# One-hot matrices over 80 nodes instead of 128, address loads moved in the first layer, and more tiles copied in place of gathered

## The chip, the cores and the metric

The kernel runs on one core of one Trainium2 chip. The metric is the device time of one execution in microseconds (us). Five engines of the core work side by side, each on its own queue of instructions, and meet only at semaphores: TensorE (PE, matmuls and transposes), VectorE (DVE), ScalarE (ACT), GpSimd (POOL, which here only issues gathers) and SyncE (SP, which issues the plain transfers). Times are compared with three runs of the kernel before.

## The reference, cut to what matters

Two graph layers over 12,500 nodes with 128 features, and 200,000 edges that are sorted by their target node. All of it is 32-bit floating point.

```python
# layer 0
h = relu(layernorm(x))
agg = segment_sum(h[src], dst, 12500)          # sum of the sources of each node's edges
x = x + (agg @ W_rel.T + b_rel + h @ W_root.T)
# layer 1
h = relu(layernorm(x))
w = silu(edge_features @ We1 + be1) @ We2 + be2   # one vector of 128 for each edge
agg = segment_sum(h[src] * w, dst, 12500)
x = x + h + (silu(agg @ Wn1 + bn1) @ Wn2 + bn2)
```

## The kernel before, in words

**Groups and tiles.** The edges are cut into 196 groups of 1024, and a group into 8 tiles of 128 edges (one edge for each partition). Each layer walks the groups in order. Because the edges are sorted by target, the 1024 edges of a group go to few neighbouring nodes: with the inputs of the reference the widest group spans 72 of them. The kernel takes a window of `W` nodes from the first target of the group on, and checks on the chip that no edge lies outside it (a slow second program follows if one does).

**Sum over edges.** For each group VectorE compares the targets with the numbers 0 to `W`-1 (`compare`, line 278) and so makes a one-hot matrix `oh` of 128 edges by `W` nodes for each tile. PE multiplies each tile of source rows `hs` (the weights) by its one-hot matrix (line 391) and accumulates the 8 tiles in one bank: 128 features by `W` nodes. In the profile each of these 32-bit products stands as two matmuls and two weight loads. VectorE adds the bank to the sums `both` at the window's place (`add`, line 409), whose address comes from a register.

**Source rows: gathered or copied.** POOL gathers the rows of a tile by index from chip memory (`fetch`, line 265, one instruction for one tile), into one of 6 buffers `hs`. It may not start on a buffer before the scatter that read it 6 groups ago is done. Some tiles are not gathered. The transposed table of all nodes lies in `both`, a node to a column; ScalarE and VectorE copy 128 columns, one instruction for one column of 128x4 bytes, into a tile `hc` (lines 608 and 606; three such tiles), PE transposes it (`turn`, line 633), and ScalarE copies the result into `hs` (`place`, line 639). I call this a helped tile. `HELP` tells how many: in layer 0 one in each group (from group 18 on, after a start in which the first rows are normalized as they come), in layer 1 nine in ten groups. `HC` splits the 128 columns: in layer 0 VectorE takes 60 and ScalarE 68, in layer 1 56 and 72. The tile's columns are copied four groups (`HW`) ahead of the group that needs it.

**Addresses.** The place of each column is read into registers, up to 16 (`HL`) with one load instruction on the engine that copies (`take`, line 591); then follow the copies (`put`). In layer 1, `hook` lets VectorE issue one such load right behind the compare, one behind the addition of line 376 and one behind the product of line 380, so that they run beside these; the copies come later, in `spread`. In layer 0 there are no hooks: `spread` alternates loads and copies behind `add`.

**Layer 1.** For each group PE makes the hidden layer of the edges (`hidden`, line 355), ScalarE its silu (line 358), PE the weights of the messages (`weigh`, line 368), VectorE adds a bias (line 376) and multiplies by the source rows (line 380); then comes the scatter of line 391. PE's order in one step is hidden of group g+2, scatter of g, weigh of g+1, then a `turn` and node work.

**Node work.** As soon as the sums of 512 nodes (a batch; there are 25) are complete, their dense part is done between the groups: in layer 0 matmuls of lines 471 and 475, statistics on VectorE (lines 483, 289, 292) and ScalarE (294, 308); in layer 1 lines 545, 547, 555 to 564.

**What sets the order.** All semaphores and the order on each engine are written out by hand; `beside` and `plan` place the node work and the turns behind certain groups. An engine executes strictly in this order, so a wait on an engine holds all behind it.

Of the kernel before, what the change touches and what calls it, by code (L numbers as in the profile page):

```python
# [20 lines left out]
D = 128  # L21
GT = 8
GE = GT * P
W = 128
WG = 512
GL = 4
NB = 4
# [4 lines left out]
XB = 4  # L32
FB = 4
EP = 51
HELP = ((1, 1), (9, 10))
HC = (60, 56)
HW = 4
TABLE = 16512
HL = 16
# [27 lines left out]
def helped(n_nodes, n_edges):  # L67

    ng = n_edges // GE
    nbt = len(last_groups(n_nodes, n_edges))
    layers = []
    for begin, (tiles, groups) in ((min(ng, -(-nbt // 2) + FB) + 1, HELP[0]), (1, HELP[1])):
        ends = (begin - 1 - -(i + 1) * groups // tiles for i in range(ng * tiles // groups))
        layers.append((begin, [(e + HW, e) for e in ends if e + HW < ng - 1]))
    return layers


# [21 lines left out]
def kernel(  # L102
# [41 lines left out]
    FG = min(NG, -(-NBT // 2) + FB)  # L144
    places, blocks = help_places(N, n_edges)
    helps = [
        (layer, h, e, begin, j)
        for layer, (begin, groups) in enumerate(helped(N, n_edges))
        for j, (h, e) in enumerate(groups)
    ]  # L150
    helped_groups = {(layer, h) for layer, h, *_ in helps}

    def rows_of(ap, n0, rows, nt):
        return ap[n0 : n0 + rows * nt, :].rearrange("(t p) d -> p t d", p=rows)
# [36 lines left out]
    with (  # L191
# [64 lines left out]
        def fetch(layer, g):  # L256

            k = layer * NG + g
            at(G, done["src", 0 if g < 8 else 1], done.get(("ap", k - (HB if g < NG - 8 else LB))))
            if layer:  # L260
                at(G, *(done["h1 out", b] for b in range(max(0, NBT - 2), NBT)))
            elif g >= FG:
                at(G, *(done["h0 out", b] for b in range(max(0, NBT - 3), NBT)))
            for t in range(tiles_of[g] - ((layer, g) in helped_groups)):
                ins = G.indirect_dma_start(  # L265
                    out=hs[k % HB][:, t, :], out_offset=None,
                    in_=h1_d if layer else x if g < FG else h0_d,
                    in_offset=bass.IndirectOffsetOnAxis(
                        ap=src_sb[:, g * GT + t : g * GT + t + 1], axis=0
                    ),  # L270
                )
                done["hs", k] = inc(ins, f"hs{k % HB}", 16)
# [339 lines left out]
        def spread(layer, g):  # L612

            for taken in hooked:
                put(V, taken)
            hooked.clear()
            for engine, rest in ((V, hooks), (A, list(chunks(layer, g, A)))):
                for chunk in rest or (chunks(layer, g, V) if engine is V and not layer else ()):
                    put(engine, take(engine, chunk))
            hooks.clear()  # L620

# [10 lines left out]
            at(T, done["b3"] if layer else done.get(("placed", i - 2)), done["table", NBT - 1])  # L632
            done["tile", i] = inc(T.transpose(bank, hc[i % 3], ident), "pe")  # L633

        def place(i, layer, h):
# [3 lines left out]
            done["hx", k] = done["placed", i] = inc(A.copy(hs[k % HB][:, GT - 1, :], bank), "act")  # L639
            if layer:  # L640
                done["b3"] = done["placed", i]

        with tc.tile_critical():
# [112 lines left out]
            for i, (layer, h, e, begin, j) in enumerate(helps):  # L756
# [6 lines left out]
                if not layer:  # L763
                    plan(0, e + 2, lambda i=i, h=h: place(i, 0, h))
            placed = {e + 1: (i, 1, h) for i, (layer, h, e, *_) in enumerate(helps) if layer}
# [8 lines left out]
            for layer in range(2):  # L774
                fetch(layer, 0)
                if layer:
                    weigh(0)
                else:
                    done["oh", 0] = inc(compare(0, 0), "dve")
                for g in range(NG):  # L780
                    k = layer * NG + g
                    if g + 1 < NG:
                        fetch(layer, g + 1)
                    if not layer:
                        if g + 1 < NG:
# [12 lines left out]
                    else:  # L798
                        if g:
                            add(1, g - 1)  # L800
                        if 2 * EG <= g + 3 < NG and (g + 3) % EG == 0:
                            load(g + 3)
                        if g + 2 < NG:
                            hidden(g + 2)
                        scatter(1, g)
                        hooks.extend(chunks(1, g, V))
                        if g + 1 < NG:
                            weigh(g + 1)
                    for what in beside[layer].get(g, ()):
                        what()  # L810
                    spread(layer, g)
                    if layer and g in placed:
                        place(*placed[g])
                add(layer, NG - 1)
                for what in beside[layer].get(NG, ()):
                    what()
# [191 lines left out]
```

## Time and profile before

| | us |
|---|---|
| kernel before, median of 3 runs (4913.62 to 4926.87) | 4920.62 |
| the profiled execution | 4865.67 |
| its span, first to last instruction | 4863.9 |
| layer 0 from group 18 on, and layer 1 without its ends: the stretches read below | 400 to 2200, 2600 to 4600 |
| ScalarE busy | 3051.0 (63%) |
| VectorE busy | 2750.9 (57%) |
| GpSimd busy | 2629.1 (54%) |
| PE matmuls busy | 2554.6 (53%) |

A line of the grouped view holds line, engine, operation, tiles written and read, shapes, count; then busy time and mean duration in ns of one; then the engine's idle time just before these instructions and what ended it. "issue" means that nothing that the profile shows was waited for. A line of the timeline holds start, duration, what was done and how often, and in brackets the idle time before it. PEclk is the granted TensorE clock as a share of the full one.

### The profile page before, as it was taken

Reading aid. Unit: us, or ns where it says so; the run is one execution under the profiler, and the core shown is the slowest. Engines: PE = TensorE matmul, PEld = TensorE weight load, DVE = VectorE, ACT = ScalarE, POOL = GpSimd, SP = SyncE. Lnnn points to the kernel's source line nnn. Section 1 sums busy time; section 2 is a strip of 40 time slices with the busy share of each in tenths; the row PEclk is TensorE's granted clock in tenths of the full one; section 3 lists DMA queues with packets and bytes.
Section 4 is the critical chain, followed back from the end, with each engine's and each line's share of the span. In section 5 each row is a group of like instructions: output and inputs, shape, how many; then the busy total and the mean of one; then the engine's idle time right before and its main releaser. Section 6 shows DMA issues by size and latency. Waiting matters only on the chain.

```text
span 4863.9 us, 77667 instructions
## 1 busy us (share of the span) xinstructions
PE 2554.6 (53%) x11440; PEld 1986.8 (41%) x11440; DVE 2750.9 (57%) x21943; ACT 3051.0 (63%) x24975; POOL 2629.1 (54%) x2791
## 2 busy tenths in 40 slices
PE   2433333333333333334456767677666776667777
PEld 1423333332332333333344545455444554444555
DVE  3545555555455555555256566666655665666665
ACT  4646656666666666667356666666666666666664
POOL 6655555555555555554555455555554555555544
PEclk9666655566556666656677777777777777777778
DMA  3411111111111111111122222212221222222221
GB/s 109 112 49 50 51 43 47 47 52 46 44 45 53 45 45 53 47 47 43 52 63 58 59 62 63 59 55 61 64 58 55 59 61 59 63 61 61 58 57 48
DMA packets 187106, 275.72 MB, mean 57 GB/s; under 512 B 48331, under 2 KB 136658, under 8 KB 181586
## 3 DMA queue, kind: packets, MB, share of 16 engines
q0 software_dynamic: 89088, 182.63, 14.5%
q1 hardware_dynamic: 97300, 87.96, 5.9%
q14 instruction: 429, 3.51, 0.2%
q8 instruction: 93, 1.52, 0.1%
q10 hardware_dynamic: 196, 0.09, 0.0%
HBM read 244.89 MB, written 25.60 MB: 56 GB/s over the span
## 4 chain that ended last, share of the span: by engine, by line
ACT 33%; issue 28%; DVE 16%; PE 11%; another core or an unknown queue 8%; ACTq 3%; DVEq 1%; SPq 0%; DMA 0%
ACT hc L608 28%; DVE hc L606 9%; PE bank L391 4%; ACT hid L358 3%; PE pair L355 3%; ACTq L591 3%; DVE oh L278 2%; PE pair L368 2%; DVEq L591 1%; DVE stn L289 1%; ACT hs L639 1%; PE bank L475 1%; DVE st L289 0%; DVE hs L380 0%
## 5 line engine op out<-in xcount | busy, mean ns | idle before, releaser
L265 POOL DMA_INDIRECT hs<-h_d,src_sb x2648 | 2499.4, 944 | 2137.2 <-PE bank L391 1119.3
L608 ACT COPY hc<-both 128x4 uint8 x23936 | 2596.6, 190 | 1364.9 <-issue 1344.9
L606 DVE TENSOR_TENSOR hc<-both,bank 128x4 uint8<-128x4 uint8 x19840 | 1588.2, 150 | 1238.9 <-issue 1226.3
L391 PE MATMUL bank<-oh,hs 128*128 128x128 f32 x6252 | 1268.7, 386 | 291.1 <-issue 120.1
L391 PEld LDWEIGHTS bank<-oh,hs 128*128 128x128 f32 x6252 | 1194.4, 294 | 525.5 <-issue 264.2
L633 PE MATMUL pair<-ident,hc 128*128 128x128 f32 x172 | 73.0, 424 | 1281.1 <-ACT hc L608 411.5
L355 PE MATMUL pair<-ef,we_sb 50*128 50x512 f32 (+1 forms) x782 | 549.8, 837 | 75.8 <-ACT hid L358 33.5
L633 PEld LDWEIGHTS pair<-ident,hc 128*128 128x128 f32 x172 | 30.4, 176 | 1318.9 <-issue 778.5
L278 DVE TENSOR_TENSOR oh<-bank,rel 128x1024 f32<-128x1024 f32 x392 | 475.0, 1212 | 16.9 <-issue 16.7
L376 DVE TENSOR_TENSOR pair<-pair,be_sb 128x1024 f32<-128x1024 f32 x196 | 240.3, 1226 | 407.6 <-PE pair L368 214.9
L368 PE MATMUL pair<-we_sb,hid 128*128 128x128 f32 x3126 | 441.6, 302 | 4.7 <-issue 4.7
L368 PEld LDWEIGHTS pair<-we_sb,hid 128*128 128x128 f32 x3126 | 434.9, 222 | 3.0 <-issue 3.0
L358 ACT ACTIVATE hid<-pair,be_sb 128x1024 f32<-128x1024 f32 x196 | 217.1, 1108 | 105.5 <-remote 58.9
L355 PEld LDWEIGHTS pair<-ef,we_sb 50*128 50x128 f32 x782 | 172.7, 244 | 260.2 <-issue 222.4
L380 DVE TENSOR_TENSOR hs<-pair,hs 128x1024 f32<-128x1024 f32 x196 | 239.3, 1221 | 17.6 <-DMA hs<-h_d,src_sb 8.1
L633 PE MATMUL bank<-ident,hc 128*128 128x128 f32 x170 | 58.6, 345 | 353.6 <-remote 87.1
L633 PEld LDWEIGHTS bank<-ident,hc 128*128 128x128 f32 x170 | 26.2, 154 | 391.6 <-issue 137.9
L265 POOL DMA_INDIRECT hs<-in_x,src_sb x136 | 128.5, 945 | 73.2 <-issue 40.2
L409 DVE TENSOR_TENSOR both<-both,bank 128x128 f32 x392 | 109.0, 278 | 71.8 <-remote 47.1
L483 DVE TENSOR_TENSOR bank<-bank,xt 128x512 f32<-128x512 f32 (+1 forms) x25 | 17.2, 689 | 153.7 <-PE bank L475 52.9
L294 ACT ACTIVATE sdn<-mvn,eps 128x4 f32<-128x4 f32 (+1 forms) x50 | 14.9, 298 | 125.0 <-DVE mvn L292 45.6
L555 PE MATMUL bank<-bn_r,ones_r 1*128 1x512 f32 (+1 forms) x50 | 37.8, 845 | 90.0 <-remote 60.7
(69 smaller groups left out, 888.9 us busy)
## 6 DMA issues: line engine op xcount, KB each, us to landing
hs<-h_d,src_sb POOLq DMA_INDIRECT x2648
ef<-in_ef_t SPq DMA_DIRECT2D x98, 408.0 KB
xt<-in_x SPq DMA_DIRECT2D x48, 256.0 KB
h_d<-h SPq DMA_DIRECT2D x48, 256.0 KB
keep_d<-xt SPq DMA_DIRECT2D x24, 256.0 KB
xt<-keep_d SPq DMA_DIRECT2D x24, 256.0 KB
out_x<-xt SPq DMA_DIRECT2D x24, 256.0 KB
hs<-in_x,src_sb POOLq DMA_INDIRECT x136
```

Source lines behind the costliest of these rows:

```text
L265: ins = G.indirect_dma_start(out=hs[k % HB][:, t, :], out_offset=None, in_=h1_d if layer else x if g < FG else h0_d, in_offset=bass.Indire ...
L278: return V.tensor_tensor(oh[k % OB][:, :n, :], io.unsqueeze(1).to_broadcast([P, n, W]), rel[:, g, :n].unsqueeze(2).to_broadcast([P, n, W]) ...
L355: ins = T.matmul(hp_b[:, c : c + m], we1_sb, e[:, c : c + m], start=True, stop=True)
L358: ins = A.activation(hid[g % 2][:, :n], hp_b[:, :n], AF.Silu, bias=be1_sb)
L368: ins = T.matmul(wp[:, t, :], hid[g % 2][:, t * P : (t + 1) * P], we2_sb, start=True, stop=True)
L376: ins = V.tensor_add(w, w, be2_sb.unsqueeze(1).to_broadcast([P, n, D]))
L380: done["msg", g] = inc(V.tensor_mul(h, w, h), "dve")
L391: ins = T.matmul(ap[k % AB], hs[k % HB][:, t, :], oh[k % OB][:, t, :], start=(t == 0), stop=(t == tiles_of[g] - 1),)
L591: _, columns = nc.values_load_multi_w_load_instructions(help_at[row : row + 1, block, lo:hi], engines=[kind], min_val=TABLE, max_val=TABLE ...
L606: ins = V.tensor_tensor(to, column, zero_b, ALU.bitwise_or)
L608: ins = A.copy(to, column)
L633: done["tile", i] = inc(T.transpose(bank, hc[i % 3], ident), "pe")
```

## The change

The window shrinks from 128 to 80 nodes: `oh`, the bank and the addition are over 80 columns, and so is the moving side of the scatter's matmuls. In layer 0, VectorE's chunks of columns are handed to the hooks before the compare of the next group, and one address load is issued right behind that compare, ahead of `add`; the rest is as before. The helped tiles go from 1 in each group to 11 in ten groups in layer 0 (so that in each tenth group two of the eight tiles are copied and six gathered) and from 9 in ten to 19 in twenty groups in layer 1. The split becomes 64 and 64 columns in layer 0, 60 (VectorE) and 68 (ScalarE) in layer 1. `slot` counts which tile from the end of the group a helped tile is.

```diff
-W = 128
+W = 80
-HELP = ((1, 1), (9, 10))
-HC = (60, 56)
+HELP = ((11, 10), (19, 20))
+HC = (64, 60)
...
-        ends = (begin - 1 - -(i + 1) * groups // tiles for i in range(ng * tiles // groups))
-        layers.append((begin, [(e + HW, e) for e in ends if e + HW < ng - 1]))
+        ends = [begin - 1 - -(i + 1) * groups // tiles for i in range(ng * tiles // groups)]
+        slots = [ends[:i].count(e) for i, e in enumerate(ends)]
+        layers.append((begin, [(e + HW, s, e) for s, e in zip(slots, ends) if e + HW < ng - 1]))
...
-            for t in range(tiles_of[g] - ((layer, g) in helped_groups)):
+            for t in range(tiles_of[g] - helped_groups.count((layer, g))):
...
-                for chunk in rest or (chunks(layer, g, V) if engine is V and not layer else ()):
+                for chunk in rest:
...
-            done["hx", k] = done["placed", i] = inc(A.copy(hs[k % HB][:, GT - 1, :], bank), "act")
+            done["hx", k] = done["placed", i] = inc(A.copy(hs[k % HB][:, GT - 1 - slot, :], bank), "act")
...
                     if not layer:
+                        hooks.extend(chunks(0, g, V))
                         if g + 1 < NG:
                             compared = compare(0, g + 1)
+                            hook()
```

Counted in the two programs: 189 helped tiles instead of 172 in layer 0 and 179 instead of 170 in layer 1, 2758 gathers instead of 2784, 22,836 column copies on VectorE instead of 19,840 and 24,268 on ScalarE instead of 23,936, 1711 address loads on VectorE instead of 1405 and 1788 on ScalarE instead of 1767.

More of the change, by code (lines that the diff above doesn't have):

```diff
@@ L146 @@
     helps = [
-        (layer, h, e, begin, j)
+        (layer, h, slot, e, begin, j)
         for layer, (begin, groups) in enumerate(helped(N, n_edges))
-        for j, (h, e) in enumerate(groups)
+        for j, (h, slot, e) in enumerate(groups)
     ]
-    helped_groups = {(layer, h) for layer, h, *_ in helps}
+    helped_groups = [(layer, h) for layer, h, *_ in helps]
     def rows_of(ap, n0, rows, nt):
@@ L633, in turn, with place @@
             done["tile", i] = inc(T.transpose(bank, hc[i % 3], ident), "pe")
-        def place(i, layer, h):
+        def place(i):
+            layer, h, slot, *_ = helps[i]
             bank = b3[:, :P] if layer else tp[i % 2][:, 0, :]
@@ L755 @@
                 plan(1, ready[0] - 1, lambda b=b: node_load(b, keep_d))
-            for i, (layer, h, e, begin, j) in enumerate(helps):
+            placed = {}
+            for i, (layer, h, _, e, begin, j) in enumerate(helps):
                 tiles, groups = HELP[layer]
@@ L762 @@
                 plan(layer, e + 1, lambda i=i, layer=layer: turn(i, layer))
-                if not layer:
-                    plan(0, e + 2, lambda i=i, h=h: place(i, 0, h))
-            placed = {e + 1: (i, 1, h) for i, (layer, h, e, *_) in enumerate(helps) if layer}
+                if layer:
+                    placed[e + 1] = i
+                else:
+                    plan(0, e + 2, lambda i=i: place(i))
             plan(0, FG, check_a)
@@ L812 @@
                     if layer and g in placed:
-                        place(*placed[g])
+                        place(placed[g])
                 add(layer, NG - 1)
@@ L969, in by_tile @@
         return np.pad(v, (0, pad), constant_values=fill).reshape(-1, P).T
-    helps = [h for _, groups in helped(a["x"].shape[0], n_edges) for h, _ in groups]
+    helps = [
+        (h + 1) * GT - 1 - slot
+        for _, groups in helped(a["x"].shape[0], n_edges)
+        for h, slot, _ in groups
+    ]
     places, blocks = help_places(a["x"].shape[0], n_edges)
     help_t = np.zeros((P, blocks[-1], P), np.int32)
-    for place, h in zip(places, helps):
-        help_t[place] = a["src"][(h + 1) * GE - P : (h + 1) * GE]
+    for place, t in zip(places, helps):
+        help_t[place] = a["src"][t * P : (t + 1) * P]
     arrays = {
```

## Prediction

> **What bounds the kernel now.** I read the windows view first, to set the two layers apart, then each engine's groups in each layer with the idle time before them, then a timeline.
>
> ```profile
> 400.00:2200.00 1800.00, 647.58 (x2987) 585.47 (x2986) 983.28 (x9528) 1167.05 (x10464) 989.16 (x1050) 0.61 0.18 47
> 2600.00:4600.00 2000.00, 1385.22 (x6103) 990.72 (x6104) 1234.08 (x8668) 1311.07 (x10636) 1063.00 (x1128) 0.74 0.22 60
> ```
>
> The columns are the stretch, then busy time of PE, weight loads, VectorE, ScalarE, GpSimd, then the granted clock. No engine is busy over 70%. Layer 0 has 150 compares in this stretch, 12.0 us a group; layer 1 has 159, 12.6 us a group. The groups of ScalarE and VectorE in layer 0:
>
> ```profile
> L608 ACT COPY hc<-both 128x4 uint8 x10200 | 1107.2, 190 | 575.8 <-issue 567.1
> L294 ACT ACTIVATE sdn<-mvn,eps 128x4 f32<-128x4 f32 x19 | 5.6, 297 | 37.1 <-DVE stn L289 16.7 <-DVE mvn L292 15.6 <-issue 4.7
> ```
>
> ```profile
> L606 DVE TENSOR_TENSOR hc<-both,bank 128x4 uint8<-128x4 uint8 x9000 | 735.5, 150 | 674.8 <-issue 668.3
> L278 DVE TENSOR_TENSOR oh<-bank,rel 128x1024 f32<-128x1024 f32 x150 | 182.4, 1216 | 14.8 <-issue 14.8
> L409 DVE TENSOR_TENSOR both<-both,bank 128x128 f32 x150 | 41.2, 275 | 0.0
> L483 DVE TENSOR_TENSOR bank<-bank,xt 128x512 f32<-128x512 f32 x19 | 13.3, 700 | 116.7 <-remote 46.5 <-PE bank L475 45.5 <-issue 24.7
> ```
>
> ScalarE is busy 1167 us and idle 567 us before column copies for nothing that is shown; real waits come to some 40 us. So its 12 us are full. VectorE has the same kind of idle time and really waits only at L483 (117 us, 0.78 us a group). Counted off tile by tile (60 copies on VectorE and 68 on ScalarE make one), ScalarE finished last in all 172 tiles of layer 0, at the median by some 4 us. ScalarE sets layer 0.
>
> In layer 1:
>
> ```profile
> L608 ACT COPY hc<-both 128x4 uint8 x10314 | 1121.2, 190 | 604.4 <-issue 595.9
> L358 ACT ACTIVATE hid<-pair,be_sb 128x1024 f32<-128x1024 f32 x159 | 176.5, 1110 | 19.2 <-issue 11.8 <-PE pair L355 7.2
> L639 ACT COPY hs<-bank 128x128 f32<-128x128 f32 x143 | 36.6, 256 | 11.1 <-issue 11.0
> L547 ACT ACTIVATE hid<-bank,bn_sb 128x512 f32<-128x512 f32 x20 | 13.7, 687 | 54.5 <-PE bank L545 33.1 <-remote 14.9 <-PE pair L368 3.3
> ```
>
> ```profile
> L376 DVE TENSOR_TENSOR pair<-pair,be_sb 128x1024 f32<-128x1024 f32 x159 | 195.5, 1230 | 281.7 <-PE pair L368 177.7 <-issue 51.6 <-remote 35.3
> ```
>
> Again ScalarE is the fullest, with 85 us of waits (L547, L358, L639) for PE. VectorE has room: 282 us of waiting at L376.
>
> The idle time called "issue" is the odd part. A timeline of layer 1 shows what goes with it:
>
> ```profile
> 3666.60 0.38 ACT L608 COPY hc<-both 128x4 uint8 x3 [1.14 <-issue]
> 3668.04 0.19 ACT L608 COPY hc<-both 128x4 uint8 x1 [0.52 <-issue]
> ...
> 3669.76 6.44 ACT L608 COPY hc<-both 128x4 uint8 x64
> ...
> 3680.01 0.69 ACT L547 ACTIVATE hid<-bank,bn_sb 128x512 f32<-128x512 f32 x1 [2.63 <-PE bank L545]
> ```
>
> ```profile
> 3666.97 0.94 POOL L265 DMA_INDIRECT hs<-h_d,src_sb  x1 [0.31 <-issue]
> 3677.59 0.94 POOL L265 DMA_INDIRECT hs<-h_d,src_sb  x1 [9.68 <-PE bank L391]
> ```
>
> ```profile
> 3669.66 0.45 PE L633 MATMUL bank<-ident,hc 128*128 128x128 f32 x1 [8.49 <-DVE hc L606]
> 3670.04 3.78 PE L355 MATMUL pair<-ef,we_sb 50*128 50x512 f32 x4
> 3673.75 3.57 PE L391 MATMUL bank<-oh,hs 128*128 128x128 f32 x16
> 3677.16 1.95 PE L368 MATMUL pair<-we_sb,hid 128*128 128x128 f32 x16
> ```
>
> While gathers run, the copies come in ones and threes with steps of 0.7 us; while GpSimd pauses, 64 columns take 6.44 us, 0.101 us each, addresses included. In all such runs of seven gathers the copies go freely during the first three or four and stall some 80% of the time during the rest and 1.5 us after. So the last gather of a run costs both copying engines about 1 us each.
>
> **The change part by part**, for each group.
>
> *ScalarE, layer 0.* 11/10 tiles of 64 columns are 70.4 instead of 68: 2.4 x 0.101 = +0.24. A tenth more of a place (L639, 0.26 us): +0.03. A tenth less of a gather: from its mean share (567 us by 1050 gathers, 0.54 us) to its whole 1.25 us step; I take 1.0, since it is the last of a run that goes: -0.10. [...] The rows show ScalarE stalling with the gathers, and I follow them. Sum +0.17, by 172 groups **+29 us**.
>
> *VectorE, layer 0.* 70.4 columns instead of 60, at 0.072 us (32 in 2.29 us in the same timeline, GpSimd idle): +0.75. Its loads of addresses go from 4.0 to 5.2 a group; one that isn't covered shows as a gap of 0.54 us: +0.65. The first load now lies beside the compare; before, it was uncovered in about a third of the groups, for 0.77 us: -0.27. It is also ahead of `add`'s wait now; it waits for nothing itself, and nothing but `add` stands behind it. The compare over 640 instead of 1024 elements: L278 takes 1.216 us and 512 elements took 0.70 (L483), so 0.82: -0.40. The addition over 80: from 275 to some 225 ns, -0.05. Gather -0.10. Sum +0.58. It is hidden by the 4 us by which VectorE is ahead and by its 0.78 us at L483; 0.2 us of rate is left. If that cover fails, up to 0.58 x 172 = 100 us come. I take 0.1 us a group: **+17 us**.
>
> *PE.* The scatter's 16 matmuls ran cold in 3.57 us, 223 ns each; warm ones of the same shape (L368) took 122. With 80 instead of 128 columns streamed the cold ones would take 139: -1.34 us; the other end is nothing, if the weight loads, which stay 128x128, set the pace. [...] I take 0.8 us a scatter.
>
> Where does it go? In layer 0 PE mostly stands at L633 for ScalarE's columns; what a faster scatter gives is that the sums of a batch (L475, then L483, then L294) come sooner: L294's wait is 37.1 / 19 = 2 us a batch, and 22 batches lie here: **-18 us**. In layer 1, L547 waits 54.5 / 20 = 2.7 us a batch behind hidden, scatter and weigh: 24 x 0.8 = **-19 us**. L358 and L639 wait 30 us in this stretch, 36 in the layer; a third: **-12 us**. The wait at L376 is VectorE's and doesn't count while ScalarE is full.
>
> *Layer 1, the rest.* ScalarE copies 64.6 columns instead of 64.8 (-0.02) and a twentieth of a gather goes (-0.05): 0.07 x 191 = **-13 us**. VectorE: 6.6 columns more, +0.48; compare and addition -0.45; half a load more, mostly under the three hooks, +0.1: inside its 1.8 us a group at L376.
>
> *Start.* 17 groups, bound by gathers of 8 tiles and by the normalization; 0.2 us each: **-4 us**. The pause between the layers and the last groups have no helped tiles and stay.
>
> Sum: 29 + 17 - 18 - 19 - 12 - 13 - 4 = **-20 us** on the profiled 4865.67. That execution is 1.1% under the median of the runs; the same difference on 4920.62 gives **4900 us**.
>
> **The rivals.**
>
> *VectorE becomes the bound of layer 0* (18%). It takes on 0.58 us a group and has 0.78 of waiting, part of which can't go: after a batch's sums PE needs scatter and L471 to L475, 5 us or more behind the turn. It decides from the point where VectorE's columns end last. Then all 0.58 us count, 100 us in place of 29 + 17 - 18: +52 us, 4973. For it: 1.2 more loads and 10.4 more columns. Against it: it was never last in 172 tiles.
>
> *The scatter gets no faster, or its gain isn't passed on* (14%): weight loads bind. The PE terms go (49 us): +29, 4950.
>
> *PE's order is the loop of layer 1* (18%). The timeline has PE 8.5 us at L633 and then four steps one after the other, with VectorE (6 us) and GpSimd (9.7 us) behind it. If a sooner scatter releases all, half of the 0.8 us counts in 195 groups, -78 in place of -31, and 0.2 us in layer 0, -34 in place of -18: -83, 4837; with the full cold gain, 4790. Against it: ScalarE is at 95% with its stalls.
>
> *It does next to nothing* (8%): all within 15 us.
>
> **How the numbers follow.** The case that I summed has 42%: 4900, its own range 4855 to 4930 (ends of the PE term and of the last gather). Within 0.3%, some 15 us, is about what a measurement of this kernel can't tell from no change. Of the summed case six in ten lie below 4906 and nearly all others in the band. Faster: 0.42 x 0.62 + 0.18 + 0.02 = 0.46. Slower: 0.18 + 0.13 + 0.02 = 0.33. Same: 0.21. The range from 4810 to 4985 leaves out the far ends of the PE loop and of a bound VectorE.
>
> **What would show it.** Right: ScalarE still last in nearly all tiles of layer 0; L608's idle time per gather as before, its copies up by 332; L391's 16 matmuls in some 2.2 us when cold; L278 at about 0.82 us; L547's and L294's idle time down by a third; layer 0 at 12.0 to 12.2 us a group, layer 1 at 12.3. Wrong: VectorE last in layer 0 and PE's L633 released by L606; matmuls of L391 still 220 ns apart; gathers that run on without pauses, so that the stalls no longer clear.

## The result, and the profile after

| | before | after |
|---|---|---|
| median of 4 runs each, us | 4917.29 (4913.62 to 4926.87) | 5056.52 (5045.29 to 5076.2) |
| ratio of the medians, 95% interval | | 1.0284 (1.0243 to 1.0326): slower |
| the profiled execution, us | 4865.67 | 5046.45 |
| its span, us | 4863.9 | 5044.3 |
| layer 0, us a group | 11.83 | 12.62 |
| layer 1, us a group | 12.50 | 12.71 |

The last two rows are the distance between the additions of two groups (18 and 190 in layer 0, 2 and 188 in layer 1), over the number of groups between. 172 groups by 0.79 us are 136 us, 186 by 0.21 are 39: together 175 of the 180 us by which the spans differ. The profiled execution of before was 1.1% below its median and that of after at the lower end of its runs, so the spans differ by more than the medians (180 and 139 us).

Line numbers shift by a few with each edit: the scatter is L391, L393 or L394, the column copies are L606 to L611, weigh is L368, L370 or L371, the turn L633 to L636.

The windows of the changed kernel, over the same two stretches (columns as before: PE, weight loads, VectorE, ScalarE, GpSimd, granted clock):

```profile
400.00:2200.00 1800.00, 676.94 (x2808) 592.56 (x2808) 984.35 (x10446) 1137.98 (x10211) 923.50 (x977) 0.51 0.17 44
2600.00:4600.00 2000.00, 1492.81 (x6035) 1114.22 (x6033) 1225.01 (x9619) 1289.70 (x10459) 1047.62 (x1108) 0.68 0.21 59
```

The clock fell, 0.61 to 0.51 and 0.74 to 0.68, and PE was busier for less work: 1493 us instead of 1385 in layer 1. Layer 0 has 141 groups in its stretch instead of 150, one in 12.77 instead of 12.0 us.

The groups of ScalarE, VectorE and PE in layer 0 (400 to 2200 us) after the change:

```profile
L610 ACT COPY hc<-both 128x4 uint8 x9947 | 1080.2, 190 | 561.2 <-issue 553.2
L296 ACT ACTIVATE sdn<-mvn,eps 128x4 f32<-128x4 f32 x18 | 5.3, 297 | 85.7 <-DVE mvn L294 63.6 <-issue 11.8 <-DVE stn L291 10.3
```

```profile
L608 DVE TENSOR_TENSOR hc<-both,bank 128x4 uint8<-128x4 uint8 x9948 | 809.8, 150 | 681.7 <-issue 666.8 <-PE bank L393 5.6 <-remote 2.8
L280 DVE TENSOR_TENSOR oh<-bank,rel 128x640 f32<-128x640 f32 x141 | 115.3, 817 | 21.9 <-issue 21.9
L411 DVE TENSOR_TENSOR both<-both,bank 128x80 f32 x141 | 33.1, 234 | 24.5 <-issue 21.9 <-PE pair L635 0.9 <-DVE hc L608 0.3
L485 DVE TENSOR_TENSOR bank<-bank,xt 128x512 f32<-128x512 f32 x18 | 12.6, 700 | 67.3 <-PE bank L477 29.3 <-issue 20.9 <-PE pair L635 7.5
```

```profile
L393 PE MATMUL bank<-oh,hs 128*128 128x80 f32 x2256 | 503.1, 416 | 384.9 <-DVE both L411 237.0 <-remote 62.6 <-issue 46.7
L635 PE MATMUL pair<-ident,hc 128*128 128x128 f32 x156 | 68.2, 437 | 658.6 <-remote 260.0 <-ACT hc L610 187.5 <-ACT hs L642 131.7
```

The same two rows of the kernel before, not shown until now; its scatter has no wait at all:

```profile
L391 PE MATMUL bank<-oh,hs 128*128 128x128 f32 x2400 | 511.4, 402 | 0.0
L633 PE MATMUL pair<-ident,hc 128*128 128x128 f32 x151 | 64.1, 424 | 1126.9 <-ACT hc L608 338.0 <-remote 335.8 <-ACT hs L639 335.2
```

Three readings. PE's scatter now waits 237 us (1.7 us a group) for VectorE's addition, where before PE stood only at the turn; PE's wait at both together is about as long (1127 us before, 1044 after), so it is who ends the wait that has changed. (The kernel waits there for one VectorE semaphore that stands for the addition and for the compare ahead of it.) ScalarE waits 85.7 us instead of 37.1 for the statistics, which VectorE makes too. And the scatter over 80 columns takes as long as over 128 (mean record 416 ns, 402 before).

In layer 1, two rows of PE, for before (first, 2600 to 4600 us) and after (2700 to 4700 us):

```profile
L391 PE MATMUL bank<-oh,hs 128*128 128x128 f32 x2544 | 493.2, 372 | 105.2 <-issue 63.3 <-DVE hs L380 41.8
L368 PE MATMUL pair<-we_sb,hid 128*128 128x128 f32 x2544 | 357.1, 301 | 0.0
```

```profile
L393 PE MATMUL bank<-oh,hs 128*128 128x80 f32 x2512 | 505.1, 384 | 152.2 <-issue 90.5 <-DVE hs L382 61.3
L370 PE MATMUL pair<-we_sb,hid 128*128 128x128 f32 x2515 | 475.7, 368 | 0.0
```

By the group (16 matmuls), weigh went from 2.25 to 3.03 us although nothing in it was changed, and the scatter, which was to get faster, from 3.10 to 3.22. The timeline shows one such pair at its place, 3.70 us where the prediction wanted some 2.2:

```profile
3670.09 3.70 PE L393 MATMUL bank<-oh,hs 128*128 128x80 f32 x16
3673.59 2.76 PE L370 MATMUL pair<-we_sb,hid 128*128 128x128 f32 x16
```

Of ScalarE's waits in layer 1 that the prediction wanted down by a third (2700 to 4700 us), L549 fell from 54.5 to 43.8 us and L360 rose from 19.2 to 29.4; with the place (11.1 to 8.3) they make 81.5 us instead of 84.8:

```profile
L549 ACT ACTIVATE hid<-bank,bn_sb 128x512 f32<-128x512 f32 x19 | 13.1, 687 | 43.8 <-PE bank L547 34.9 <-issue 9.0
L360 ACT ACTIVATE hid<-pair,be_sb 128x1024 f32<-128x1024 f32 x157 | 174.4, 1111 | 29.4 <-PE pair L357 15.1 <-issue 14.1
```

### The profile page after: what moved, and what is told of

It reads as the page before. It is cut to its first block, busy times and chain, and to the rows that moved or that the text cites. A ratio compares the mean times of both kernels' runs of the same rounds, so it can differ in the third digit from the quotient of the medians.

```text
span 5044.3 us, 81390 instructions
## 1 busy us (share of the span) xinstructions
PE 2805.0 (56%) x11466; PEld 2218.8 (44%) x11466; DVE 2812.5 (56%) x24939; ACT 3090.0 (61%) x25333; POOL 2611.6 (52%) x2765
## 4 chain that ended last, share of the span: by engine, by line
issue 27%; DVE 26%; ACT 19%; PE 16%; another core or an unknown queue 8%; DVEq 2%; ACTq 1%; SPq 0%; DMA 0%
DVE hc L608 16%; ACT hc L610 16%; PE bank L393 6%; PE pair L357 3%; PE pair L370 3%; DVE oh L280 2%; ACT hid L360 2%; DVEq L593 2%; DVE pair L378 2%; DVE hs L382 2%; ACTq L593 1%; PE bank L477 1%; DVE stn L291 1%; DVE both L411 1%
## 5 line engine op out<-in xcount | busy, mean ns | idle before, releaser
L610 ACT COPY hc<-both 128x4 uint8 x24268 | 2633.7, 190 | 1419.5 <-issue 1401.2
L608 DVE TENSOR_TENSOR hc<-both,bank 128x4 uint8<-128x4 uint8 x22836 | 1816.0, 150 | 1270.8 <-issue 1241.6
L393 PE MATMUL bank<-oh,hs 128*128 128x80 f32 x6252 | 1327.1, 400 | 822.5 <-DVE both L411 276.0
L393 PEld LDWEIGHTS bank<-oh,hs 128*128 128x128 f32 x6252 | 1260.8, 308 | 1075.2 <-issue 809.7
L370 PE MATMUL pair<-we_sb,hid 128*128 128x128 f32 x3126 | 594.2, 369 | 3.8 <-ACT hid L360 3.2
L370 PEld LDWEIGHTS pair<-we_sb,hid 128*128 128x128 f32 x3126 | 573.0, 282 | 2.0 <-issue 1.9
L280 DVE TENSOR_TENSOR oh<-bank,rel 128x640 f32<-128x640 f32 x392 | 319.2, 815 | 35.2 <-issue 34.7
L360 ACT ACTIVATE hid<-pair,be_sb 128x1024 f32<-128x1024 f32 x196 | 217.2, 1108 | 134.8 <-remote 82.3
L411 DVE TENSOR_TENSOR both<-both,bank 128x80 f32 x392 | 91.3, 233 | 92.5 <-issue 42.8
L477 PE MATMUL bank<-w_rel_sb,both 128*128 128x128 f32 x196 | 49.7, 432 | 73.1 <-DVE both L411 65.6
L477 PEld LDWEIGHTS bank<-w_rel_sb,both 128*128 128x128 f32 x196 | 44.0, 328 | 77.6 <-DVE both L411 68.6
```

The source lines that it names most:

```text
L280: return V.tensor_tensor(oh[k % OB][:, :n, :], io.unsqueeze(1).to_broadcast([P, n, W]), rel[:, g, :n].unsqueeze(2).to_broadcast([P, n, W]) ...
L360: ins = A.activation(hid[g % 2][:, :n], hp_b[:, :n], AF.Silu, bias=be1_sb)
L370: ins = T.matmul(wp[:, t, :], hid[g % 2][:, t * P : (t + 1) * P], we2_sb, start=True, stop=True)
L393: ins = T.matmul(ap[k % AB], hs[k % HB][:, t, :], oh[k % OB][:, t, :], start=(t == 0), stop=(t == tiles_of[g] - 1),)
L608: ins = V.tensor_tensor(to, column, zero_b, ALU.bitwise_or)
L610: ins = A.copy(to, column)
```

## The experiments

**A word on the chips.** All runs from here on fell on three chips where the kernel before takes 3514 to 3516 us, not 4917. Which chip the first comparison had isn't on record, so whether the chip makes this difference isn't known. On these three ScalarE's column copies hardly stall beside gathers: in a whole profile of before, ScalarE was idle 63 us ahead of its column copies (1365 us in the first comparison). GpSimd gathers without pause, one tile in 1.25 us, and the chain of waits runs along it (62% of c3_before's). Each ratio below is against the kernel before on the same chip. I come back to what this means for the first comparison.

The measured times together, in us:

| kernel | layer 0 a group | layer 1 a group | median | ratio (95%) |
|---|---|---|---|---|
| before (c3_before, one run) | 8.72 | 8.91 | 3515.56 | |
| e1_w80 | 8.77 | 9.03 | 3532.95 | 1.0046 (1.0031 to 1.0062) |
| e2_help | 9.37 | 8.88 | 3607.54 | 1.0254 (1.0236 to 1.0272) |
| e3_hook | 8.76 | 8.89 | 3516.19 | 0.9999 (0.9990 to 1.0008) |
| e4_stream128 | 9.02 | 8.84 | 3539.90 | 1.0066 (1.0049 to 1.0082) |
| a5_after (the change) | 9.00 | 9.18 | 3607.61 | 1.0264 (1.0243 to 1.0284) |
| a6_nohook | 9.17 | 9.21 | 3637.30 | 1.0333 (1.0311 to 1.0355) |
| a7_l0help_back | 8.76 | 9.23 | 3580.71 | 1.0163 (1.0114 to 1.0211) |
| a8_cmp80_stream128 | 8.75 | 8.90 | 3515.24 | 0.9999 (0.9990 to 1.0007) |
| b1_l1_one_each | 8.76 | 8.86 | 3501.32 | 0.9964 (0.9949 to 0.9979) |
| b2_two_hooks | 9.09 | 8.84 | 3554.24 | 1.0113 (1.0095 to 1.0131) |
| b3_two_hooks_l1 | 9.10 | 8.91 | 3559.74 | 1.0131 (1.0113 to 1.0149) |
| b4_split56 | 8.68 | 8.85 | 3485.85 | 0.9919 (0.9901 to 0.9937) |
| c1_split56_w80 | 8.70 | 9.18 | 3561.07 | 1.0136 (1.0120 to 1.0153) |
| c2_help_split56 | 8.67 | 8.88 | 3480.23 | 0.9901 (0.9884 to 0.9917) |

### The three parts alone

Each of the three parts of the change alone, in the kernel before: the window, the counts and the split, the place of the load. The expectations of this round were put down in the times of the first comparison, before the other chips were known; read them as ratios to 4917 us.

```diff
 e1_w80
-W = 128
+W = 80
 e2_help
-HELP = ((1, 1), (9, 10))
-HC = (60, 56)
+HELP = ((11, 10), (19, 20))
+HC = (64, 60)
 e3_hook
+                        hooks.extend(chunks(0, g, V))
                         if g + 1 < NG:
                             compared = compare(0, g + 1)
+                            hook()
```

> The kernel before with the window of 80 nodes alone; helped tiles, split and loads as before. Clock theory (the scatter's pace is set by its weight loads, 213 ns apart cold[...] with 80 columns as with 128, and the fewer columns streamed only lower the granted clock): granted clock 0.51 to 0.55 in layer 0 and 0.68 in layer 1, 4960 to 5010 us. VectorE theory (the added copies and loads are the cause): 4870 to 4900 us, since VectorE saves 0.45 us a group here. Load-order theory (the address load ahead of the addition delays the scatter): same, 4870 to 4900 us.

> The kernel before with the helped tiles and the split of the changed kernel alone (11 in ten groups and 19 in twenty, 64/64 and 60/68 columns); window 128, loads behind the addition. VectorE theory: VectorE takes 0.9 us a group more in layer 0 and has 0.8 of waiting, 5000 to 5060 us, most of it in layer 0, and PE waits for the addition. Clock theory: 4910 to 4940 us with the clock as before. Load-order theory: 4910 to 4940 us.

> The kernel before with the address load of layer 0 moved behind the compare, ahead of the addition, alone. Load-order theory: 4960 to 5050 us, all of it in layer 0, with idle time of VectorE before the addition. Clock and VectorE theories: 4880 to 4925 us.

The load's place alone does nothing (0.9999), against the load-order theory. The copied tiles alone cost 2.5%, all of it in layer 0: +0.65 us a group, and layer 1 is the same; that is what the VectorE theory expected. The smaller window costs 0.5%, most of it in layer 1: the clock fell (0.65 to 0.53 in layer 0 and 0.87 to 0.78 in layer 1, c3_before against e1_w80), as the clock theory had it, but its price was half of what that theory asked or less (1.009 to 1.019).

To see why the copied tiles cost, I take PE's scatter row in layer 0 (400 to 1600 us), first in the kernel before, then with the tiles alone, each with GpSimd's row of the same stretch:

```profile
L393 PE MATMUL bank<-oh,hs 128*128 128x128 f32 x2203 | 481.4, 407 | 260.3 <-DMA hs<-h_d,src_sb 253.0 <-DVE both L411 5.8 <-DVE hc L608 1.0
L267 POOL DMA_INDIRECT hs<-h_d,src_sb x962 | 907.6, 943 | 293.2 <-issue 291.4 <-PE pair L635 1.8
```

```profile
L393 PE MATMUL bank<-oh,hs 128*128 128x128 f32 x2053 | 466.8, 420 | 386.0 <-DVE both L411 328.6 <-DVE rsn L301 57.4
L267 POOL DMA_INDIRECT hs<-h_d,src_sb x901 | 850.0, 943 | 351.7 <-issue 257.8 <-PE bank L393 68.6 <-PE pair L635 24.9
```

Before, PE waits for gathers. With more columns on VectorE it waits for VectorE's addition, 328.6 us instead of 5.8: VectorE comes to the addition of a group later, behind the columns it copies, and a scatter needs a bank that such an addition has freed. GpSimd then waits for the scatters (68.6 us), and its 962 gathers in the stretch become 901. This is the rival "VectorE becomes the bound of layer 0". That the cause is VectorE's columns and not the copied tiles as such is shown further down, by c2_help_split56.

### The window apart from the one-hot's work

`oh` and the banks are 128 columns wide again, with 48 columns of zeros that are written once; compare and addition stay at 80. What PE streams is that of before, and VectorE's work that of the change. e4_stream128 does it to the changed kernel, a8_cmp80_stream128 to before.

```diff
+SW = 128
...
-        oh = many(OB, [P, GT, W], "oh")
+        oh = many(OB, [P, GT, SW], "oh")
...
-                oh[k % OB][:, :n, :],
+                oh[k % OB][:, :n, :W],
...
+            for t in oh:
+                V.memset(t[:, :, W:], 0.0)
```

> The changed kernel, but PE streams 128 columns of which the last 48 are zero; the compare and the addition stay at 80. Clock theory: clock back to 0.60 and 0.74, most of the loss gone, 4910 to 4960 us. VectorE and load-order theories: nothing comes back, 5030 to 5070 us.

> The kernel before with the compare and the addition over 80 nodes, but 128 columns streamed by PE (48 of them zero). Clock theory: clock as before (0.60 to 0.65 and 0.74 to 0.84), VectorE 0.45 us a group freer, 0.985 to 1.001 of before; the window alone, which streamed 80, was 1.0046. If it was the sums and not the clock: 1.0046 again.

e1_w80 and a8_cmp80_stream128 differ only in the columns that PE streams (and ran on two chips, where the kernel before takes 3515.99 and 3515.21 us). The windows of e1_w80, then of a8_cmp80_stream128:

```profile
400.00:1600.00 1200.00, 627.68 (x2714) 556.57 (x2715) 780.54 (x8650) 973.22 (x9508) 907.45 (x960) 0.53 0.24 65
1900.00:3400.00 1500.00, 1348.91 (x6377) 1035.83 (x6378) 1159.18 (x9074) 1271.32 (x11076) 1134.36 (x1200) 0.78 0.30 84
```

```profile
400.00:1600.00 1200.00, 603.48 (x2737) 531.53 (x2737) 782.59 (x8663) 973.86 (x9516) 906.91 (x962) 0.65 0.23 65
1900.00:3400.00 1500.00, 1220.50 (x6515) 922.89 (x6515) 1179.60 (x9245) 1293.14 (x11322) 1133.65 (x1203) 0.88 0.30 85
```

With fewer columns the granted clock is lower, 0.53 against 0.65 and 0.78 against 0.88, and PE is busier by 128 us in layer 1 for fewer matmuls. The same holds over all experiments and the three chips: the mean granted clock of a run is 0.65 to 0.69 wherever 80 columns are streamed, and 0.73 to 0.77 wherever it is 128. So the smaller stream doesn't shorten a matmul (mean record of the scatter in layer 1, 1900 to 3400 us: 345 ns in e1_w80, 336 in a8_cmp80_stream128); it lowers the clock and lengthens the others (weigh 351 ns against 296, hidden 675 against 636). In layer 0, where PE has room (busy 628 of 1200 us in e1_w80), this costs nothing measurable here (8.77 us a group against 8.75). In the whole change it costs layer 1: 9.18 us a group (a5_after) against 8.84 (e4_stream128), 195 groups by 0.34 or 66 us, which is the whole difference of the two medians (68 us). With that, e4_stream128 fits neither theory alone: three quarters of the loss come back, all in layer 1, and layer 0 stays slow. The chain of waits in layer 1, by line, of e4_stream128 and then of a5_after:

```profile
by line: POOL hs L268 44.5%; issue 15.7%; PE bank L394 7.2%; DVE hc L609 5.2%; DMA hs<-h_d,src_sb 4.8%; ACT hc L611 4.4%; PE pair L371 4.2%; DVE hs L383 3.6%; PE pair L358 3.1%; DVE pair L379 2.3%; DVEq L594 0.7%; PE bank L548 0.7%; DVE oh 
```

```profile
by line: PE bank L393 18.6%; PE pair L370 17.5%; DVE hc L608 13.1%; ACT hc L610 12.7%; DVE hs L382 9.1%; DVE pair L378 8.2%; PE pair L357 5.4%; issue 3.0%; DVEq L593 1.8%; DVE oh L280 1.6%; ACT hid L360 1.3%; PE bank L547 1.2%; ACTq L593 1.
```

The gathers (44.5% of the chain in e4_stream128) are no longer among its shown lines in a5_after, and the loop of PE and VectorE (scatter, weigh, bias and product: 18.6, 17.5, 8.2 and 9.1%) takes it over, with the column copies (13.1 and 12.7%). The 48 columns cost more here than alone (0.34 us a group against 0.13, from a8_cmp80_stream128 to e1_w80). VectorE copies more columns in layer 1 now, and they stand in this loop; that this is the reason I argue and didn't isolate. The rival that PE's order is the loop of layer 1 was right about the loop; but it was to go faster, and went slower. a8_cmp80_stream128 shows that the shorter compare and addition bring nothing either where gathers set the time (0.9999).

### The change again, and one part undone

The changed kernel itself; without the load behind the compare; and with layer 0's tiles back at one a group (VectorE again 60 columns there and 60 in layer 1).

```diff
 a6_nohook
                             compared = compare(0, g + 1)
-                            hook()
 a7_l0help_back
-HELP = ((11, 10), (19, 20))
-HC = (64, 60)
+HELP = ((1, 1), (19, 20))
+HC = (60, 60)
```

> The changed kernel itself, beside its parts on one chip. If the parts add up (VectorE too full in layer 0, as the window left at 128 streamed columns showed: 1.0066; and the lower clock in layer 1, which the window alone showed as 0.14 us a group): 1.012 to 1.018 of the kernel before where the gathers set the pace, as in the last comparison; 1.024 to 1.033 where the copies stall, as in the first. Clock 0.53 and 0.75 in the layers in the one case, 0.51 and 0.68 in the other.

> The changed kernel with the loads of layer 0 behind the addition again. VectorE theory: VectorE is full in layer 0, the load beside the compare hides up to 0.3 us a group, so taking it away makes it 0.5 to 1.5% slower than the changed kernel. Load-order theory: the load ahead of the addition delays it (40 to 50 us of idle time before the addition in the changed kernel), so this is 0.5 to 1% faster than the changed kernel.

> The changed kernel with one helped tile in each group of layer 0 and the split 60/68 there, as before; layer 1 as changed (19 in twenty, 60/68), window 80, load moved. VectorE theory: what layer 0 lost through the copies comes back; where the gathers set the pace 1.003 to 1.008 of before (the clock's share alone), where the copies stall 1.00 to 1.015. Clock theory (most of the loss is PE's): no more than a third comes back, 1.010 or above where the gathers set the pace, 1.02 or above where the copies stall.

The change loses by nearly the same ratio on these chips (1.0264) as in the first comparison (1.0284), but that is chance: here layer 0 lost some 47 us and layer 1 some 52, there 136 and 39. It is also more than the 1.012 to 1.018 that I had got by adding up the parts; they don't add. Without the early load it is 30 us slower still, 9.17 against 9.00 in layer 0: once VectorE sets the layer, the load's place counts, and the change got it right. With layer 0's tiles undone, layer 0 is back at 8.76, and what is left of the loss is layer 1 (9.23). The whole came to 1.0163 (its four runs lie between 3552 and 3589 us), not to the 1.003 to 1.008 of the VectorE theory: 27 of 92 us came back, because that theory had taken the clock's share from e1_w80, which is too small here.

The chain of layer 0 by line, kernel before and then the changed one (400 to 1600 us):

```profile
by line: POOL hs L267 64.2%; issue 21.8%; ACT hc L610 6.3%; PE bank L393 1.6%; PE bank L477 1.2%; DMA hs<-h_d,src_sb 1.1%; DVE hc L608 1.1%; PE bank L473 0.7%; ACTq L593 0.6%; ACT h L310 0.3%; DVE oh L280 0.3%; DVE stn L291 0.2%; DVE bank L
```

```profile
by line: DVE hc L608 49.7%; issue 21.2%; DVE oh L280 7.4%; PE bank L393 4.9%; DVEq L593 3.8%; PE bank L477 3.0%; DVE both L411 2.6%; DVE stn L291 1.3%; DVE bank L485 1.0%; DVEq L404 1.0%; PE pair L635 0.8%; DVE xt L514 0.8%; DVEq L411 0.5%;
```

GpSimd's gathers were the chain, and VectorE's column copies are now half of it.

### Tries to give the gain back

b1_l1_one_each copies one tile in each group of both layers; b2_two_hooks puts a second load right behind the addition in layer 0; b3_two_hooks_l1 adds to that one copied tile in each group of layer 1 (instead of 19 in twenty); b4_split56 gives 8 of VectorE's 64 columns of a tile to ScalarE. All four stream 128 columns.

```diff
 all four: as e4_stream128
 b1_l1_one_each
-HELP = ((11, 10), (19, 20))
+HELP = ((1, 1), (1, 1))
 b2_two_hooks, b3_two_hooks_l1
                             done["oh", k + 1] = add(0, g - 1)
+                            hook()
 b3_two_hooks_l1
-HELP = ((11, 10), (19, 20))
+HELP = ((11, 10), (1, 1))
 b4_split56
-HC = (64, 60)
+HC = (56, 60)
```

> Compare and addition over 80 nodes, 128 columns streamed (48 zero), address load moved; one helped tile in each group of both layers, split 64/64 and 60/68. Where the gathers set the pace (1.25 us each, back to back): layer 0 as before at 8.75 us a group, layer 1 from 7.1 to 7.0 gathers, 8.89 to about 8.75, so 3485 to 3505 us, 0.991 to 0.997 of before. If VectorE or ScalarE can't carry the tenth of a tile more in layer 1: 1.00 or above.

> The changed kernel with 128 columns streamed, and a second address load of layer 0 taken from behind the addition's place to right after it, so that two of the 5.2 loads a group lie beside other work of VectorE. VectorE theory (layer 0 waits for VectorE's addition because the uncovered loads and added columns fill it): one load less uncovered, up to 0.3 us a group; layer 0 goes from 9.02 to 8.65 to 8.85 us a group and the whole to 0.990 to 1.001 of before, from 1.0066. If it is the gathers or ScalarE: layer 0 stays at 9.0 and the whole at 1.005 to 1.008.

> Both: two loads covered in layer 0 with 11 helped tiles in ten groups, and one helped tile in each group of layer 1, 128 columns streamed. If both of the last two hold, their gains add: 0.983 to 0.994 of before. If layer 0 stays bound by VectorE: 0.998 to 1.005.

> The changed kernel with 128 columns streamed and layer 0 split 56 for VectorE and 72 for ScalarE (61.6 and 79.2 columns a group instead of 70.4 and 70.4); nothing else. VectorE theory: PE's wait for the addition (375 us with 64/64) falls to under 150 us; ScalarE takes 0.9 us a group more and has about 1 us of room, so layer 0 at 8.7 to 9.0 us a group, 0.993 to 1.005 of before. If the wait for the addition isn't VectorE's load: it stays over 300 us and the whole at 1.0066 or above.

The second load missed: it was to hide more of VectorE's loads and made layer 0 slower, 9.09 against 9.02. The waits of layer 0 from 400 to 1400 us (engine, line and what it waited for; us in all, times, longest) show that no wait went away. First e4_stream128, then b2_two_hooks:

```profile
PE bank L394 <- DVE both L412: 257.7, 80, 5.7
...
ACT sdn L297 <- DVE mvn L295: 150.0, 14, 11.6
```

```profile
PE bank L394 <- DVE both L412: 273.6, 86, 5.7
...
ACT sdn L297 <- DVE mvn L295: 158.0, 14, 12.7
```

The second load stands ahead of the node work on VectorE, for which ScalarE waits; that this is the cause of the 0.07 us I argue and didn't isolate. b3_two_hooks_l1 starts from the same layer 0, and its layer 1 gains nothing from the further tiles (8.91 against 8.84); with 1.0131 it lies outside both of its bands. b1_l1_one_each gains 0.36%, inside its band, though its layer 1 came to 8.86 and not to 8.75.

The split settled layer 0. With 56 columns for VectorE, b4_split56 has 8.68 us a group where e4_stream128 has 9.02, and it is faster than both kernels of the case (0.9919, a little better than its band). The same waits in it:

```profile
PE pair L636 <- ACT hc L611: 292.5, 83, 6.8
...
ACT sdn L297 <- DVE mvn L295: 15.4, 5, 4.0
...
PE bank L394 <- DVE both L412: 2.8, 2, 2.5
```

PE waits for ScalarE's columns instead, no longer for the addition (2.8 us), and the statistics come in time (15.4 us). A group of layer 0 now has 6.9 gathers, by 1.25 us 8.62; measured 8.68.

### The split in the change itself

c1_split56_w80 is the changed kernel with 56 columns, 80 streamed; c2_help_split56 is the kernel before (128 nodes, load in its old place) with the new counts of tiles and 56 columns.

```diff
 both
-HC = (64, 60)
+HC = (56, 60)
 c2_help_split56
-W = 80
+W = 128
...
-                            hook()
```

> The changed kernel with layer 0 split 56/72 alone; 80 columns streamed. If VectorE's share is all of layer 0's loss and the clock all of layer 1's: layer 0 at 8.65 to 8.75 us a group, layer 1 at 9.18 as in the changed kernel, together 1.009 to 1.014 of before where the gathers set the pace (the changed kernel 1.0264). If the lower clock also costs layer 0: layer 0 above 8.8. Where the copies stall: 1.00 to 1.02 against 1.0284.

> The kernel before with the helped tiles of the changed one and layer 0 split 56/72 (60/68 in layer 1); window 128, loads behind the addition. VectorE takes 61.6 columns a group instead of 60 there. VectorE theory: layer 0 at 8.65 to 8.8 us a group (9.37 with 64/64), the whole at 0.988 to 0.998 of before. If 1.0254 was the doing of the helped tiles themselves: above 1.015. Where the copies stall: 0.99 to 1.02.

> The kernel before, written from the changed one's text, for its profile on this chip. All theories: the time of the kernel before; 8.76 and 8.89 us a group, the gathers back to back, clock 0.65 in layer 0, where the gathers set the pace; 11.8 and 12.5 where the copies stall.

c1_split56_w80 and c2_help_split56 came out inside their bands. c1_split56_w80 has its layer 0 repaired (8.70) and still loses 1.4%, all in layer 1 (9.18): the smaller stream, since b4_split56, which differs from it only by streaming 128 columns, has 8.85. c2_help_split56 has the tiles of e2_help and 8 columns less on VectorE, and its layer 0 falls from 9.37 to 8.67 us: it was the columns, not the tiles. It gains 1.0% over before (0.9901), with b4_split56 (0.9919; the intervals overlap) the fastest of all. The copied tiles were worth something once their columns went to the engine with room, and they need neither the smaller window nor the moved load. The kernel c3_before is the kernel before in the changed kernel's text, for its profile there; it takes the time of before, so the rewritten text alone changes nothing.

## Why the prediction was wrong

I predicted 4900 us with a range of 4810 to 4985; it took 5056.52. Layer 0 was to lose 28 us (29 + 17 - 18) and lost 136; layer 1 was to gain 44 (19 + 12 + 13) and lost 39. Step by step:

**"ScalarE sets layer 0."** This step failed first. I had read it from who ends a tile's columns last, and that doesn't tell who holds the layer. After the change ScalarE still ended last in 177 of 189 tiles, with VectorE 2.1 us ahead at the median (4.7 before), and yet PE and ScalarE wait at VectorE's *other* work, the addition (237 us where there was no wait) and the statistics; ScalarE then ends its columns late because, as I read it, it is held up. That VectorE had become the bound is shown by the split in the later runs; for the first comparison it is read from the trace. The chain of waits shows it, and I hadn't read it by layer. Layer 0 (400 to 2200 us) of the first comparison, before:

```profile
by line: issue 32.9%; DVE hc L606 20.5%; ACT hc L608 20.3%; another core or an unknown queue 6.9%; DVE oh L278 4.1%; PE bank L391 3.2%; DVEq L591 3.0%; ACTq L591 1.9%; PE bank L475 1.2%; DVE stn L289 0.9%; DVE both L409 0.8%; ACT hs L639 0.
```

and after:

```profile
by line: issue 37.1%; DVE hc L608 31.1%; ACT hc L610 10.1%; DVE oh L280 4.1%; DVEq L593 2.8%; another core or an unknown queue 2.8%; PE bank L393 2.6%; PE bank L477 1.9%; DVE both L411 1.3%; ACTq L593 1.0%; DVE stn L291 0.9%; DVE bank L485 
```

Before the change both copying engines had equal parts of it. I read that as a tie, on one side of which the change put its load.

**VectorE's +0.58 us, taken as hidden.** Its size was about right and its cover wrong. From the rows of layer 0, over 150 and 141 groups: busy 983.28 to 984.35 us, 6.56 to 6.98 a group; idle before copies 668.3 to 666.8 us, 4.46 to 4.73. Together +0.70 (compare and addition were met: 817 and 234 ns where I had 820 and 225). Of the 0.78 us of waiting at the batch's addition that I counted as cover, only 0.30 went (67.3 us over 141 groups is 0.48). The other 0.40 is half of what the group gained (0.77), and the rest isn't broken down here. The rival with 4973 us (18%) was this, at a price still too low: it had 100 us for all 172 groups, and layer 0 lost 136.

**ScalarE's +0.17 us.** The group grew by 0.77 us over that stretch (12.0 to 12.77), and three rows of ScalarE make it up within 0.02: busy 1167.05 to 1137.98, 7.78 to 8.07 a group (+0.29); idle before its copies 3.78 to 3.92 (+0.14, where I had a gain of 0.10 for the gather that goes); the wait for the statistics 0.25 to 0.61 (+0.36). Such a sum closes for any engine, so it doesn't say that ScalarE was the cause; its largest part is a wait for VectorE.

**"L294: −18 us."** The sign was wrong. I took this wait for one on PE's sums; in the row of before it ended on VectorE's own statistics in 32 of 37 us. With a fuller VectorE it was longer (37.1 to 85.7 us).

**"I take 0.8 us a scatter."** Wrong at its root, and with it the −18, −19 and −12 us. I had put both ends down and taken the nearer to the columns; it was the other end. No run shows the 0.8 us: by the group the scatter of layer 1 took 3.10 us before and 3.22 after, and weigh, which stayed as it was, 2.25 and 3.03. Counted from the starts of the records in the first comparison, matmuls of the scatter follow each other in 213 ns on a cold PE and 112 on a warm one, with 80 columns as with 128. (The 107 ns warm in the expectation of e1_w80 isn't a pace of these records. The granted clock in the traces has just two values, half and full; cold is half, warm is full, and a mean of 0.61 says that it was full for 22% of the stretch.) The matmuls of `hidden`, with 512 columns, start 853 and 429 ns apart, 1.67 and 0.84 ns a column; by that, 128 columns would take 213 and 107 ns and 80 would take 133 and 67. So the pace measured at 128 columns (213 and 112) is nearly what the columns alone give, and at 80 it is still 213 and 112: there the columns don't set it. That the weight load of 128x128, which stays what it was, sets it is my guess and not shown: no run changed the weight loads, so another fixed cost of a matmul isn't ruled out.

**The clock.** I held it fixed, but for a slower weigh as the price of a faster scatter, an estimate of mine within the 0.8 us. The price came without the gain: in layer 1 weigh went from 2.25 to 3.03 us a group, and the clock from 0.74 to 0.68. Of the distances between weigh's records from 2700 to 4700 us, 1861 of 2373 were under 115 ns before and 799 of 2355 after. e1_w80 against a8_cmp80_stream128 shows that the columns alone do it: granted clock 0.53 against 0.65 in layer 0 and 0.78 against 0.88 in layer 1, and weigh's mean record in layer 1 351 ns against 296. By what way fewer columns lower the granted clock, no run shows.

**"A tenth less of a gather": −0.10.** In the first comparison the stalls per group grew, in the later runs there were hardly any (63 us of ScalarE in all of c3_before). The term can't be told from nothing. The stalls themselves I had put too high: counted over all 322 runs of seven gathers, ScalarE was idle for 50 to 63% of the last three gathers and 71% of the 1.25 us behind them, not for some 80%.

**Layer 1, −19, −12 and −13 us.** Together they became +39. I had read 85 us of ScalarE's waits as waits for PE; in the rows that I showed, PE ended only 44 of them (33.1 + 3.3 + 7.2). In the first comparison these waits fell by 3 us in all, ScalarE's stalls before copies rose from 3.75 to 3.93 us a group (595.9 us over 159, 617.3 over 157), and PE's and VectorE's parts of the chain rose. The chain of layer 1 before (2600 to 4600 us) and after (2700 to 4700 us):

```profile
by line: ACT hc L608 37.6%; issue 25.7%; ACT hid L358 6.2%; another core or an unknown queue 5.8%; PE pair L355 5.1%; PE bank L391 4.3%; ACTq L591 3.6%; PE pair L368 2.8%; DVE hc L606 2.1%; PE bank L545 0.9%; ACT hs L639 0.9%; DVE hs L380 0
```

```profile
by line: ACT hc L610 24.6%; issue 24.1%; PE bank L393 8.0%; PE pair L357 7.0%; DVE hc L608 6.8%; PE pair L370 5.9%; another core or an unknown queue 5.5%; ACT hid L360 4.0%; DVE pair L378 2.7%; DVE hs L382 2.6%; ACTq L593 2.3%; PE bank L547
```

Scatter, weigh and hidden make 20.9% of it instead of 12.2%.

**What stays open.** No run with one part alone was made where the copies stall as in the first comparison. Its two traces show the same signs as the runs elsewhere (PE waiting for the addition, the lower clock, VectorE on the chain), but how its 139 us divide among the parts is argued, not shown, and whether 56 columns would help there isn't known: ScalarE, which would take them, is stalled there for a third of the time. Why copies stall beside gathers there, and not on the three chips of the experiments, I couldn't find.

## What to carry to other kernels

Two engines that share a job and are both nearly full are a tie, and "which one ends last" doesn't name the bound: look at what else waits for each engine, and read the chain of waits for each stage before putting work on the one that seems ahead. Count a wait as cover only up to what can really go away (here 0.30 of 0.78 us). Before cutting a matmul's streamed columns, find out from the pace of the records whether the columns set it: a matmul with more columns gives the time of one column (here 512 columns, 853 ns at half the clock, 1.67 ns a column). Here they didn't at 80 (213 ns where 133 would follow), so the cut was worth nothing, and it cost clock (0.65 to 0.53 and 0.88 to 0.78).

## What the runs showed of the hardware

- The same program took 4917 us in the first comparison and 3515 us later, on three chips. The plainest difference in the traces is in the short copies: in the first comparison ScalarE and VectorE stall in steps of 0.7 us while gathers run (1365 us of idle time before ScalarE's copies and 1239 before VectorE's in the whole profile); in c3_before these are 63 and 314 us.
- Matmul records of 32 bits, each with its own weights of 128x128, follow each other in 213 ns where the traces show half the clock granted and in 112 ns where they show all of it, with 80 columns streamed as with 128 (the scatters of both traces of the first comparison).
- Fewer streamed columns gave a lower granted clock (0.65 to 0.53 and 0.88 to 0.78 in the two layers for 128 to 80 columns, e1_w80 against a8_cmp80_stream128, nothing else changed), and slower matmuls elsewhere (weigh's mean record in layer 1: 351 ns against 296).
- Indirect gathers of 128 rows, back to back, start every 1.25 us though each is busy for 0.944 us (c3_before, 1203 of them from 1900 to 3400 us), and there, where they are 64.2% of layer 0's chain, a group takes their time: 7 by 1.25 us is 8.75, and layer 0 took 8.72.
